# Shared small norm steps, outputs' norms on ACT, later bias additions, and K made beside P, in a macaron S4D block

## The chip, the cores and the metric

The kernel runs on one core of one Trainium2 chip. The metric is the device time of one execution in microseconds (us), taken as a median of several runs. A core has five engines that run side by side, each from its own queue in order: TensorE (PE, with its weight loads PEld), VectorE (DVE), ScalarE (ACT), GpSimd (POOL) and SyncE (SP, which here issues nearly all transfers). They meet through semaphores.

## The reference

The input x has 8 sequences of 2048 tokens with 256 features. Three sublayers follow one another, each added to its input:

```python
x = x + 0.5 * ffn(layernorm(x), w1, b1, w2, b2)
x = x + s4d(layernorm(x), log_A_real, A_imag, C_re, C_im, log_dt, D, ln_w, ln_b)
x = x + 0.5 * ffn(layernorm(x), w1, b1, w2, b2)
# ffn(x) = relu(x @ w1 + b1) @ w2 + b2, 256 -> 1024 -> 256
# s4d: K[h, l] = 2 Re sum_n Ct[h, n] exp(dt A[h, n] l);  y = causal convolution of x with K per feature
#      r = x + y + D x;  out = layernorm(r) * ln_w + ln_b
```

All of it is float32.

## The kernel before

**Stages.** There are 16384 tokens, cut into 64 groups of 256 (two tiles of 128 tokens on the partitions). The first feed-forward (tag "a") runs over the 64 groups, then comes the state-space stage, then the second feed-forward (tag "b"). The products are made to nearly float32 accuracy out of two parts of each operand (high and low, fp32r), three matmuls for one. The state-space stage works on 128-token chunks: its convolution needs the taps K of one chunk (kept in `kpad` in DRAM) and, for each batch of eight features, matrices P (kept turned in `pt_dram`) and O (`o_dram`) that take inputs into states and states into outputs.

**Steps.** `sublayer` (L821) writes out the work of a feed-forward in steps; a group has eight (`SLOTS`), one for each 128 columns of the hidden layer. In each step PE gets six matmuls of `up` (L802) and six of `down` (L812), which lags three steps (`LAG`). ACT makes the relu hx (L870) and DVE its low part (L117, hx). Around the matmuls run generators: `pre(g)` starts `lead` steps ahead (18 in "a") and makes a group's input, `post(g)` takes its output. Each `yield` in them passes one step, so the number of yields says how many steps ahead something is issued.

**An input** (`pre_a`, `ffn_in`): load x (256 KB on SP), statistics (two bn_stats, two bn_aggr on DVE), a root on ACT (`root`), two reciprocals and two small scalar_tensor_tensor q on DVE (`rstds`), nb on DVE and two normalisations into xn on ACT (`norm`, L701). POOL adds half of the output bias to x (L733). xn is then turned: for groups 14 to 18 and from 44 on by a DMA through DRAM (`turn_by_dma`, planes of 16 bits), for the others by four PE transposes (L740), after which ACT makes xh and DVE xl. Groups that PE turns load seven steps (`XL`) later than those that the DMA turns.

**An output** (`post_a`): DVE adds the down product to x (L917), SP stores it as x1, then the same chain of statistics, root, reciprocals and q, and the normalised rows go into columns of the big tile u: on ACT for groups below 12 (`ACT_NORM`), on DVE from 12 on (L705). `posted` counts the groups that are through.

**Background.** Beside the first feed-forward runs `matrices()`, a generator that yields paces in us of planned time. `fill` takes from it until its planned time has caught up with 1.32 a step (10.56 a group). It first makes the discrete parameters on DVE and powers of them on POOL (tables pa, pb), then the taps K (L499 to L556: 32 two-input steps on DVE over four rounds, 32 matmuls, and 16 small DMAs from POOL's queue), then P and O in 32 batches of eight features at a pace of 8.0 a batch: `make` on POOL (six products, L583 to L593), `spread` (two copies of 16-bit planes, one on DVE and one on ACT, L603, and stores of the planes and of O), `turn` (a transposing DMA read, pinned), `transpose` (two copies back, one on DVE and one on ACT, L629, pinned in program order, and a store). The parts of successive batches overlap, so the loop has 35 passes of six yields. Two marks have due groups: "half" (after pass 18) at group 32, since the later outputs need the room in u, and "tables" at group 48; a mark that isn't reached by then is forced, all that is left before it being issued at once. Last comes `early()`, the first part of the state-space stage.

**Order.** Within the dependencies the order on each engine is planned when the kernel is built, with program order as the priority; `keep_in_program_order` pins an instruction, and `issue_after` keeps one behind another. SP's and POOL's queues hold their DMA issues in that same order.

Of the kernel before, what the change touches and what calls it, by code (L numbers as in the profile page):

```python
# [10 lines left out]
F32 = mybir.dt.float32  # L11
# [8 lines left out]
P = 128  # L20
# [23 lines left out]
def macaron_s4d_kernel(  # L44
# [202 lines left out]
    def matrices():  # L247
# [248 lines left out]

        GP, GD = 32, 8  # L499
        vz = room[2][:, 0 : 2 * GP * 2 * NA].rearrange("p (r g c a) -> p r g c a", r=2, g=GP, c=2)  # L500
        for c in range(2):
            V.memset(vz[c * N : (c + 1) * N, :, :, 1 - c, :].rearrange("p r g a -> p (r g) a"), 0.0)
        za, zb = (
            room[2][:, i * P : (i + 2) * P].rearrange("p (g a) -> p g a", a=NA) for i in (8, 10)
        )
        mine = cells[14][:, 0:GD]
        V.tensor_reduce(
            mine, ident.rearrange("p (g x) -> p g x", g=GD), op=ALU.add, axis=mybir.AxisListType.X
        )
        prod = room[2][:, 16 * P : 20 * P].rearrange("p (q b g) -> p q b g", b=NB, g=GD)  # L510
        kev = room[2][:, 20 * P : 20 * P + (GP // GD) * NB].rearrange("p (q b) -> p q b", b=NB)
        yield S1
        for gi in range(NPAIR // GP):
            gs = slice(gi * GP, (gi + 1) * GP)
            br = pb[:, 0, gs, 0:1].to_broadcast([P, GP, NA])
            bi = pb[:, 1, gs, 0:1].to_broadcast([P, GP, NA])
            ar, ai = pa[:, 0, gs, :], pa[:, 1, gs, :]
            V.tensor_mul(za, ar, br)
            V.tensor_mul(zb, ai, bi)
            yield S2  # L520
            for c in range(2):
                cp = slice(c * N, (c + 1) * N)
                V.tensor_sub(vz[cp, 0, :, c, ::-1], za[cp], zb[cp])
            yield S2
            V.tensor_mul(za, ar, bi)
            stt(zb, ai, -1.0, br, ALU.mult, ALU.mult)
            yield S2
            for c in range(2):
                cp = slice(c * N, (c + 1) * N)
                V.tensor_sub(vz[cp, 1, :, c, ::-1], zb[cp], za[cp])  # L530
            yield S2
            pk = bank("b", f"pk{gi}")
            for q in range(GP // GD):
                for ri in range(2):
                    nc.tensor.matmul(
                        pk[:, q * P : (q + 1) * P],
                        vz[:, ri, q * GD : (q + 1) * GD].rearrange("p g c a -> p (g c a)"),
                        pb[:, ri, gi * GP + q * GD : gi * GP + (q + 1) * GD, :],
                        start=(ri == 0),
                        stop=(ri == 1),  # L540
                    )
                yield 1.3
            V.tensor_mul(
                prod,
                pk.rearrange("p (q g b) -> p q b g", g=GD, b=NB)[:, :, ::-1, :],
                mine.unsqueeze(1).unsqueeze(1).to_broadcast([P, GP // GD, NB, GD]),
            )
            yield 1.3
            V.tensor_reduce(kev, prod, op=ALU.add, axis=mybir.AxisListType.X)
            yield 1.3  # L550
            for q in range(GP // GD):
                h0 = 2 * (gi * GP + q * GD)
                nc.gpsimd.dma_start(
                    out=kpad[h0 : h0 + 2 * GD, 0:P].rearrange("h (a b) -> h a b", b=NB),
                    in_=kev[:, q, :],
                )  # L556


        first = NBT // 2
# [36 lines left out]
        def spread(bt):  # L596

            pl = planes[:, bt % 2]
            pu = p_of(bt).bitcast(U16).rearrange("p (m w) -> p w m", w=2)
            for _ in range(DI):  # L600
                yield
            for w in range(2):
                P_DEINT[w](pl[:, w], pu[:, w])  # L603
            yield
            via = pv_dram[bt % 2]
            nc.sync.dma_start(out=via, in_=pl.rearrange("p w m -> p (w m)"))
            yield
            nc.sync.dma_start(out=o_dram[bt], in_=p_of(bt))
            yield
# [24 lines left out]
            yield  # L634

        planes = wpool.tile([P, 2, 2, BCH * P], U16, name="planes", tag="wE")
        P_DEINT = (V.tensor_copy, A_.copy)
        P_REINT = (V.tensor_copy, A_.copy)
        PY = 0
        BACK = 3  # L640
        DI = 2
        PX = 2
        PA = 8.0
        PB_ = 8.0
        PPIN = 1

        for bt in range(NBT + BACK):
            parts = []
            if 0 <= bt - BACK < NBT:
                parts.append(transpose(bt - BACK))  # L650
            if 0 <= bt - 2 < NBT:
                parts.append(turn(bt - 2))
            if 0 <= bt - 1 < NBT:
                parts.append(spread(bt - 1))
            if bt < NBT:
                parts.append(make(bt))
            for n in range(6):
                for p in parts:
                    next(p, None)
                yield (PA if bt <= first else PB_) / 6  # L660
            if bt == first + BACK - 1:
                yield "half"
        yield "tables"
# [1 line left out]

    x1_dram = dram.tile([P, NJ * B, H], F32, name="x1_dram")

    def stats(srcs, name, pin=False):
        st = stat.tile([P, NTB, 6], F32, name=f"st_{name}", tag="st")
        mv = stat.tile([P, NTB, 2], F32, name=f"mv_{name}", tag="mv")  # L670
        for i, src in enumerate(srcs):
            ins = V.bn_stats(st[:, i, :], src)  # L672
            if pin:
                tc.keep_in_program_order(ins)
        for i in range(NTB):
            V.bn_aggr(mv[:, i, :], st[:, i, :])
        return mv

    def root(mv, name):

        s = stat.tile([P, NTB], F32, name=f"s_{name}", tag="s")
        A_.activation(s, mv[:, :, 1], AF.Sqrt, bias=eps4, scale=0.25)  # L682
        return s

    def rstds(mv, s, name):

        t = stat.tile([P, NTB], F32, name=f"t_{name}", tag="tt")
        q = stat.tile([P, NTB], F32, name=f"q_{name}", tag="q")
        V.reciprocal(t, s)
        stt(q, mv[:, :, 1], EPS, t, ALU.add, ALU.mult)  # L690
        stt(q, q, 0.25, s, ALU.mult, ALU.add)
        V.reciprocal(t, q)
        return t

    def norm(dsts, srcs, mv, rs, name, on_act=False):
        if on_act:
            nb = stat.tile([P, NTB], F32, name=f"nb_{name}", tag="nb")
            stt(nb, mv[:, :, 0], -1.0, rs, ALU.mult, ALU.mult)
        for i, (dst, src) in enumerate(zip(dsts, srcs)):
            if on_act:  # L700
                A_.activation(  # L701
# [16 lines left out]
    def halves(xt):  # L718
        return [xt[:, i, :] for i in range(NTB)]

    def ffn_in(xt, name, on_act=False, by_dma=False):

        mv = stats(halves(xt), f"f{name}", PINF)
        yield
        s = root(mv, f"f{name}")
        yield
        rs = rstds(mv, s, f"f{name}")
        yield
        norm(
            [xn[:, i, 0 : H - 1] for i in range(NTB)], [xt[:, i, 0 : H - 1] for i in range(NTB)],  # L730
            mv, rs, f"f{name}", on_act,
        )
        G_.tensor_add(xt, xt, hb2.unsqueeze(1).to_broadcast([P, NTB, H]))  # L733
        yield
        if by_dma:
            return (yield from turn_by_dma(xn, name))
        pt = bank("t", f"pt_{name}")
# [83 lines left out]
    def sublayer(w1t, w2t, pre, post, lead, tag, first=(), background=(), due=()):  # L821
# [9 lines left out]
        last = {}  # L831

        def step():
            for key in list(running):
                try:
                    next(running[key])
# [59 lines left out]

    LAG = 3
    pend = {}
    posted = [0]
    xts = {}  # L900


    ACT_NORM = 12

    def pre_a(g):
        by_dma = g >= DMA_A and not DMA_X <= g < DMA_Y
        for _ in range(0 if by_dma else XL):
            yield
        xt = xts[g] = slot("x", [P, NTB, H], f"xa_{g}")
        nc.sync.dma_start(out=xt, in_=hbm(x, g))  # L910
        for _ in range(XY):
            yield
        return (yield from ffn_in(xt, f"a{g}", True, by_dma))

    def post_a(g, po):
        xt = xts.pop(g)
        V.tensor_add(xt, po, xt)  # L917
        yield
        nc.sync.dma_start(out=x1_dram[:, g * NTB : (g + 1) * NTB, :], in_=xt)
        mv = stats(halves(xt), f"u{g}")  # L920
        yield
        s = root(mv, f"u{g}")
        yield
        rs = rstds(mv, s, f"u{g}")
        norm(ucols(g), halves(xt), mv, rs, f"u{g}", g < ACT_NORM)
        yield
        yield
        posted[0] = g + 1

# [155 lines left out]
    def early():  # L1085
# [41 lines left out]
    nc.gpsimd.dma_start(out=hb2, in_=b2.partition_broadcast(P))  # L1127
    G_.tensor_scalar_mul(hb2, hb2, 0.5)
    sublayer(
        w1t, w2t, pre_a, post_a, 11 + XL, "a", load_weights(), chain(matrices(), early()),  # L1130
        {"half": NG // 2, "tables": NG * 3 // 4},
    )

# [27 lines left out]

    def pre_b(g):
        by_dma = g >= DMA_B
        for _ in range(0 if by_dma else XL):
            yield
        xt = xts[g] = slot("x", [P, NTB, H], f"xb_{g}")
        i0 = g * NTB
# [21 lines left out]
    def post_b(g, po):  # L1189
# [7 lines left out]
        )  # L1197

    sublayer(
        [wb1[:, i] for i in range(2)], [wb2[:, i] for i in range(2)], pre_b, post_b, 12 + XL, "b"  # L1200
    )


# [30 lines left out]
```

## Time and profile before

| what | value |
|---|---|
| median of 3 runs | 1845.31 us (1841.72 to 1846.10) |
| the profiled execution's own time | 1843.95 us |
| its span, first to last instruction | 1842.2 us |
| mean granted TensorE clock | 0.98 |
| first feed-forward, relus of "a" | 20.9 to 854.5 us |
| second feed-forward, first to last `up` of "b" | 1094.3 to 1834.4 us |
| matmuls of each feed-forward | 6144 |

The page gives, for each engine, the time with an instruction in work, in all and in 40 equal slices of 46 us (each digit is a share in tenths). A row of a group reads: line, engine, operation, output <- inputs, shape, count, then busy us, mean ns of one, and the engine's idle time just before with what ended it. The idle time of an engine that isn't the bound costs nothing. A duration is that of an instruction in work, waits for a port included; instructions of one engine can overlap a little.

### The profile page before, as it was taken

What the parts mean: (1) busy time and instruction counts of PE and PEld (TensorE: products, weight loads), DVE (VectorE), ACT (ScalarE), POOL (GpSimd) and SP (SyncE); (2) the same over time, 40 slices, a digit from 0 to 9 for tenths busy, and PEclk for the clock granted to TensorE, in tenths of its full rate; (3) what the DMA queues carried; (4) which work ended last, traced back from release to release, by engine and by line L of the source; (5) the groups of instructions that cost most, each with busy time, mean ns of one, the idle gap of its engine ahead of it and who ended that gap; (6) DMA issues with size and microseconds to landing.
All of it is one profiled execution on the core that took longest, in us unless ns stands there. A gap on an engine that the chain in (4) does not pass through costs nothing. (4 is left out here: it accounts for less than half of the span.)

```text
span 1842.2 us, 41540 instructions
## 1 busy us (share of the span) xinstructions
PE 1747.9 (95%) x15147; PEld 1715.8 (93%) x15147; DVE 1492.6 (81%) x4919; ACT 925.2 (50%) x2139; POOL 713.7 (39%) x964
## 2 busy tenths in 40 slices
PE   6999799998998999999989879999999999999999
PEld 5999799988998999998888879999999999999998
DVE  5999897888899867765999947888888888888875
ACT  4455334554655655553545425555555555555553
POOL 1116851888587414111778612222222222222220
PEclk9999899998999999999999979999999999999999
DMA  5112132787888933334878833333332333333332
GB/s 203 47 47 56 52 111 77 241 237 227 247 250 246 247 110 90 101 105 137 253 232 235 256 115 87 93 89 92 88 100 85 91 98 87 98 89 90 94 95 55
DMA packets 299696, 246.39 MB, mean 134 GB/s; under 512 B 169954, under 2 KB 242402, under 8 KB 298978
## 3 DMA queue, kind: packets, MB, share of 16 engines
q1 hardware_dynamic: 297456, 241.75, 45.2%
q8 instruction: 119, 1.95, 0.4%
q10 hardware_dynamic: 1266, 1.31, 0.2%
q0 software_dynamic: 768, 0.66, 0.2%
q14 instruction: 87, 0.71, 0.1%
HBM read 92.93 MB, written 111.15 MB: 111 GB/s over the span
## 5 line engine op out<-in xcount | busy, mean ns | idle before, releaser
L812 PE MATMUL po_a<-wa,hx_a 128*128 128x256 f32 x3072 | 457.1, 287 | 17.4 <-DVE hx_a L117 17.1
L802 PE MATMUL ph_a<-xh_a,wa 128*128 128x256 f32 x2048 | 460.2, 289 | 5.2 <-ACT xh_a L749 3.5
L802 PE MATMUL ph_b<-xh_b,wb 128*128 128x256 f32 x2048 | 443.2, 284 | 2.5 <-ACT xh_b L749 2.4
L812 PE MATMUL po_b<-wb,hx_b 128*128 128x256 f32 x3072 | 441.2, 283 | 0.3 <-DVE hx_b L117 0.3
L812 PEld LDWEIGHTS po_a<-wa,hx_a 128*128 128x128 f32 x3072 | 407.7, 194 | 23.4 <-DVE hx_a L117 22.4
L812 PEld LDWEIGHTS po_b<-wb,hx_b 128*128 128x128 f32 x3072 | 400.5, 192 | 0.5 <-DVE hx_b L117 0.5
L802 PEld LDWEIGHTS ph_a<-xh_a,wa 128*128 128x128 f32 x2048 | 361.3, 196 | 6.8 <-ACT xh_a L749 3.9
L802 PEld LDWEIGHTS ph_b<-xh_b,wb 128*128 128x128 f32 x2048 | 352.8, 193 | 3.6 <-ACT xh_b L749 3.0
L802 PE MATMUL ph_a<-xl_a,wa 128*128 128x256 f32 x1024 | 294.1, 290 | 23.4 <-DVE xl_a L751 20.6
L870 ACT ACTIVATE hx_b<-ph_b 128x256 fp32r<-128x256 f32 x512 | 191.6, 381 | 244.3 <-PE ph_b L802 226.6
L117 DVE SCALAR_TENSOR_TENSOR hx_a<-ph_a,hx_a 128x256 fp32r<-128x256 f32 x512 | 207.9, 412 | 127.7 <-ACT hx_a L870 126.6
L870 ACT ACTIVATE hx_a<-ph_a 128x256 fp32r<-128x256 f32 x512 | 189.0, 381 | 228.8 <-PE ph_a L802 213.6
L1169 POOL TENSOR_TENSOR xb<-xb,lnb_sb 128x512 f32<-128x512 f32 x64 | 84.0, 1315 | 523.3 <-DMA xb<-x_dram 384.4
L802 PE MATMUL ph_b<-xl_b,wb 128*128 128x256 f32 x1024 | 285.2, 284 | 0.0
L117 DVE SCALAR_TENSOR_TENSOR hx_b<-ph_b,hx_b 128x256 fp32r<-128x256 f32 x512 | 210.1, 414 | 57.3 <-ACT hx_b L870 51.7
L802 PEld LDWEIGHTS ph_a<-xl_a,wa 128*128 128x128 f32 x1024 | 201.2, 196 | 27.0 <-DVE xl_a L751 23.5
L733 POOL TENSOR_TENSOR xa<-xa,hb 128x512 f32<-128x512 f32 x64 | 85.5, 1336 | 362.4 <-ACT xn L701 328.0
L802 PEld LDWEIGHTS ph_b<-xl_b,wb 128*128 128x128 f32 x1024 | 197.4, 193 | 0.2 <-DVE xl_b L751 0.2
L701 ACT ACTIVATE xn<-xa,nb_fa,t_fa 128x255 f32<-128x255 f32 x128 | 69.7, 591 | 104.2 <-DVE nb_fa L117 82.2
L733 POOL TENSOR_TENSOR xb<-xb,hb 128x512 f32<-128x512 f32 x64 | 93.9, 1467 | 50.0 <-ACT xn L701 34.5
L701 ACT ACTIVATE xn<-xb,nb_fb,t_fb 128x255 f32<-128x255 f32 x128 | 69.9, 594 | 75.7 <-DVE nb_fb L117 72.0
L761 DVE COPY pl_b<-xn 128x512 uint16<-128x512 uint16 x62 | 42.7, 688 | 74.3 <-ACT xn L701 74.3
(264 smaller groups left out, 2773.2 us busy)
## 6 DMA issues: line engine op xcount, KB each, us to landing
xa<-in_L_attn_x_dram SPq DMA_DIRECT2D x64, 256.0 KB, 2.9
x_dram<-xa SPq DMA_DIRECT2D x64, 256.0 KB, 2.3
o<-u SPq DMA_DIRECT2D x32, 512.0 KB, 4.2
pv<-planes SPq DMA_DIRECT2D x32, 512.0 KB, 3.6
pt<-u SPq DMA_DIRECT2D x32, 512.0 KB, 3.3
tz<-kpad SPq DMA_DIRECT2D x64, 256.0 KB, 4.2
xb<-x_dram SPq DMA_DIRECT2D x64, 256.0 KB, 2.7
out_dram<-xb SPq DMA_DIRECT2D x64, 256.0 KB, 2.9
```

The costliest lines, as they stand in the source:

```text
L117: return V.scalar_tensor_tensor(out=o, in0=a, scalar=s, in1=b, op0=op0, op1=op1)
L701: A_.activation(dst, src, AF.Identity, bias=nb[:, i : i + 1], scale=rs[:, i : i + 1])
L733: G_.tensor_add(xt, xt, hb2.unsqueeze(1).to_broadcast([P, NTB, H]))
L761: copy(pl[:, w], xu[:, :, :, :, w])
L802: nc.tensor.matmul(ph, wt[wp][:, dc, fs], xp[:, dc, :], start=(n == 0), stop=(n == 3 * NDC - 1))
L812: nc.tensor.matmul(po[:, i, :], hp[:, tsl], wt[wp][:, fc, :], start=(fc == 0 and i == 0 and n == 0), stop=(fc == NFC - 1 and n == 2), skip ...
L870: last[A_] = A_.activation(hh, ph, AF.Relu)
L1169: G_.tensor_add(xt, xt, lnb_sb.unsqueeze(1).to_broadcast([P, NTB, H]))
```

## The change

Only the first feed-forward and what runs beside it are edited.

1. K's code becomes a generator `lags()`. It is no longer run ahead of P: one yield of it is taken with each of the six yields of a pass of P's loop, and its own paces aren't counted.
2. Both copies of P's deinterleave (`spread`) are on ACT, one a yield. P's paces go from 8.0 to 9.1 for the first 19 passes and to 10.3 after that.
3. From group 3 on, the statistics of an input g and those of the output g-3 lie in one tile (class `Joint`). `post_a(g-3)` makes one root, one set of reciprocals and q, and one nb for both; `ffn_in(g)` waits three yields and uses them. `post_a` has no yield any more between the addition and the store, and one between nb and the norms.
4. `ACT_NORM` goes from 12 to 52, so ACT normalises the outputs of groups 12 to 51 too.
5. With a joint, the bias addition is put into a generator of its own that waits five more steps, and is pinned in program order on POOL.
6. Inputs from group 3 on are all loaded at the same distance ahead; groups that PE turns wait two more steps after the norm instead.

The lead stays at 18 and 19, and the second feed-forward keeps its numbers.

```diff
-        GP, GD = 32, 8
...
-                nc.gpsimd.dma_start(
-                    out=kpad[h0 : h0 + 2 * GD, 0:P].rearrange("h (a b) -> h a b", b=NB),
+        def lags():
+            GP, GD = 32, 8
...
             for w in range(2):
-                P_DEINT[w](pl[:, w], pu[:, w])
-            yield
+                A_.copy(pl[:, w], pu[:, w])
+                yield
...
-        PA = 8.0
-        PB_ = 8.0
+        PA = 9.1
+        PB_ = 10.3
...
+        beside = lags()
...
                 for p in parts:
                     next(p, None)
-                yield (PA if bt <= first else PB_) / 6
+                next(beside, None)
+                yield (PA if bt < first + BACK else PB_) / 6
...
+    def shifts(mv, rs, name):
+        nb = stat.tile([P, mv.shape[1]], F32, name=f"nb_{name}", tag=f"nb{mv.shape[1]}")
+        stt(nb, mv[:, :, 0], -1.0, rs, ALU.mult, ALU.mult)
+        return nb
...
+    def ffn_in(xt, name, on_act=False, by_dma=False, joint=None):
+
+        if joint:
+            stats(halves(xt), f"f{name}", mv=joint.mv[:, 0:NTB])
+
+            for _ in range(3):
+                yield
+            mv, rs, nb = joint.mv[:, 0:NTB], joint.rs[:, 0:NTB], joint.nb[:, 0:NTB]
...
-        G_.tensor_add(xt, xt, hb2.unsqueeze(1).to_broadcast([P, NTB, H]))
-        yield
+        def add_bias():
+            return G_.tensor_add(xt, xt, hb2.unsqueeze(1).to_broadcast([P, NTB, H]))
+
+        def later():
+            for _ in range(5):
+                yield
+            tc.keep_in_program_order(add_bias())
+
+        if joint:
+            spawned.append((name, later()))
+        else:
+            add_bias()
+        yield
+        if joint and not by_dma:
+            yield
+            yield
...
-    ACT_NORM = 12
+    ACT_NORM = 52
...
+    class Joint:
+        def __init__(self, g):
+            self.mv = moments(2 * NTB, f"j{g}")
+
+    joints = {}
+    JG = 3
...
-        for _ in range(0 if by_dma else XL):
+        for _ in range(XL if g < JG else 0):
             yield
...
+        if g >= JG:
+            joints[g - JG] = Joint(g - JG)
+        return (yield from ffn_in(xt, f"a{g}", True, by_dma, joints.get(g - JG)))
...
         V.tensor_add(xt, po, xt)
-        yield
         nc.sync.dma_start(out=x1_dram[:, g * NTB : (g + 1) * NTB, :], in_=xt)
-        mv = stats(halves(xt), f"u{g}")
-        yield
-        s = root(mv, f"u{g}")
-        yield
-        rs = rstds(mv, s, f"u{g}")
-        norm(ucols(g), halves(xt), mv, rs, f"u{g}", g < ACT_NORM)
-        yield
+        joint = joints.pop(g, None)
+        mv = stats(halves(xt), f"u{g}", mv=joint.mv[:, NTB:] if joint else None)
+        whole = joint.mv if joint else mv
+        yield
+        s = root(whole, f"u{g}")
+        yield
+        rs = rstds(whole, s, f"u{g}")
+        nb = shifts(whole, rs, f"u{g}")
+        if joint:
+            joint.rs, joint.nb = rs, nb
+            rs, nb = rs[:, NTB:], nb[:, NTB:]
+        yield
+        norm(ucols(g), halves(xt), mv, rs, f"u{g}", g < ACT_NORM, nb)
         yield
         posted[0] = g + 1
```

## The prediction

> **What bounds the kernel now.** I read the page first: busy times, and the 40 slices of 46 us.
>
> ```profile
> PE 1747.9 (95%) x15147; PEld 1715.8 (93%) x15147; DVE 1492.6 (81%) x4919; ACT 925.2 (50%) x2139; POOL 713.7 (39%) x964
> ...
> PE   6999799998998999999989879999999999999999
> PEld 5999799988998999998888879999999999999998
> DVE  5999897888899867765999947888888888888875
> ACT  4455334554655655553545425555555555555553
> POOL 1116851888587414111778612222222222222220
> ```
>
> PE is the bound, but not evenly. The second feed-forward (slices 24 on) is full; the first (14 to 855 us) has holes, just where POOL's row is high. Only the first is edited, so I look at its groups. The time line has eight hx_a activations on ACT for each group of 256 tokens; the first of groups 1, 11, 15, 21, 23, 43, 44 and 48 start at 36.5, 155.3, 219.1, 300.5, 324.4, 597.1, 617.0 and 663.2 us. I asked for the busy time in these stretches:
>
> ```profile
> 36.50:155.30 118.80, 118.80 (x995) 118.44 (x995) 107.28 (x435) 59.84 (x149) 20.36 (x22) 1.00 0.15 45
> 155.30:219.10 63.80, 55.98 (x428) 54.93 (x426) 55.87 (x151) 28.18 (x70) 52.72 (x47) 0.92 0.21 63
> 219.10:300.50 81.40, 76.59 (x626) 74.86 (x627) 73.92 (x213) 31.64 (x82) 39.57 (x42) 1.00 0.24 79
> 324.40:597.10 272.70, 250.46 (x1992) 244.47 (x1991) 243.57 (x633) 148.76 (x316) 210.99 (x172) 0.97 0.80 240
> 597.10:617.00 19.90, 16.89 (x120) 16.18 (x121) 17.67 (x44) 8.90 (x19) 14.91 (x12) 0.92 0.82 235
> ```
>
> Columns: length, then busy PE, PEld, DVE, ACT, POOL, clock, DMA share, GB/s. Groups 1 to 10 take 11.88 us each with PE full, although DVE is 90% busy. The **floor** of a group is 11.52 us (the chain of waits repeats at that step in the second feed-forward), plus 0.45 for four transposes where the input isn't turned by DMA: 11.97. Groups 23 to 42, with the tables P made beside them, take 13.63 us. There I asked for the waits between 330 and 610 us (total, times, longest):
>
> ```profile
> ACT xn L701 <- DVE nb_fa L117: 61.7, 19, 5.4
> POOL xa L733 <- ACT xn L701: 33.6, 14, 10.9
> ...
> PE ph_a L802 <- DVE xl_a L751: 16.7, 12, 3.0
> ```
>
> So PE waits for DVE, ACT stands at its queue's head for nb_fa with the relus behind it, and POOL stands behind ACT. Why DVE is late shows in the groups by form, first in that window, then in 760 to 800 us, where POOL is nearly idle:
>
> ```profile
> L705 DVE TENSOR_SCALAR u<-xa,mv_u,t_u 128x256 f32<-128x256 f32 x40 | 33.3, 928 | 0.1
> L603 DVE COPY planes<-u 128x1024 uint16<-128x1024 uint16 x27 | 27.3, 1012 | 0.0
> L117 DVE SCALAR_TENSOR_TENSOR q_u<-mv_u,t_u 128x2 f32<-128x2 f32 x20 | 12.2, 612 | 0.3
> L117 DVE SCALAR_TENSOR_TENSOR q_u<-q_u,s_u 128x2 f32<-128x2 f32 x20 | 11.4, 570 | 0.2
> ```
>
> ```profile
> L705 DVE TENSOR_SCALAR u<-xa,mv_u,t_u 128x256 f32<-128x256 f32 x6 | 2.7, 550 | 0.0
> L117 DVE SCALAR_TENSOR_TENSOR q_u<-mv_u,t_u 128x2 f32<-128x2 f32 x3 | 0.5, 161 | 0.1
> ```
>
> The same step on two numbers takes 161 ns alone and 612 beside POOL. The time line shows how; nb_fa ends as POOL's operation does, and ACT, which starts 0.1 us after it, has stood 8.75 us (put down to "issue"):
>
> ```profile
> 215.04 2.97 DVE L117 SCALAR_TENSOR_TENSOR nb_fa<-mv_fa,t_fa 128x2 f32<-128x2 f32 x1
> ...
> 216.93 1.06 POOL L583 TENSOR_TENSOR u<-u 128x512 f32<-128x512 f32 x1
> ...
> 218.09 1.09 ACT L701 ACTIVATE xn<-xa,nb_fa,t_fa 128x255 f32<-128x255 f32 x2 [8.75 <-issue]
> ```
>
> **The change, part by part** (durations from 330 to 610 us, 20 groups).
>
> Shared small steps. For groups 3 on, one root, two reciprocals, two q and one nb serve an input (g) and an output (g-3) together. On DVE that takes away one q pair, 0.61 + 0.57 us, and one reciprocal pair, 0.16 + 0.14: 1.48 us a group; on ACT one root of 0.29. The steps left work on four numbers instead of two; I take the same duration. New is a wait: an input's norm now needs the outputs of group g-3. By the step counts these are added at step 8g-14, the norms run at 8g-11, and the input is used at 8g. A late nb holds ACT's head and the relus behind it; PE has three steps, 4.3 us, before it misses hx.
>
> Outputs' norms on ACT to group 51. DVE loses 2 x 0.93 = 1.86 us a group, ACT gains 2 x 0.84 = 1.68 (row of u<-xa,nb_u, 18 before 150 us). The Trainium skill, "ScalarE: Activation LUTs", Rules for kernel authors, would keep plain arithmetic off ACT; by DVE's 550 ns alone it would be right here, by the 928 beside POOL it is not, and the difference decides only the ACT rival below.
>
> Both copies of P's deinterleave on ACT: DVE loses 1.01 us, ACT gains 1.05, per batch. P's paces go from 8.0 to 9.1 and 10.3 units; a group is 8 x 1.32 = 10.56, so batches a group fall from 1.32 to 1.16, then 1.03. Groups 23 to 42 then hold 21 batches instead of 26.
>
> The bias addition waits five more steps and leaves POOL's head: the 33.6 us of POOL waits vanish. Behind it on POOL stand P's products. It comes at 8g-5 and is needed at 8g+10, 21 us on; free. If POOL were stuck behind a kpad DMA or a pt store (11.3 us of such waits in all), those 21 us still cover it.
>
> Loads of groups 3 to 13 and 19 to 43 are issued seven steps earlier, and the store of x1 one step earlier, right behind the addition. On SP the store can hold what follows (pv, planes, pt) until DVE has added; now SP waits 12.8 us in all for that addition in the 280 us. Hidden by the batch period of 10.4 us against landings of 3 to 5; uncovered it would come back as ACT's pinned waits for planes, 8.0 us now. The earlier loads cost five x buffers nothing: 31 steps of life against 40.
>
> The uniform timing also removes two bursts. Today groups 14 and 44 normalise 11 steps ahead but 13 and 43 four ahead, so two groups' inputs fall into one group's time: groups 13, 14 and 43 last 15.8, 20.9 and 19.9 us. And xl, ready one step ahead now, is ready six ahead, so the 16.7 us wait goes.
>
> K beside P. K's own pauses, 0.9 + 4 x 13.2 = 53.7 units, go, so P begins that much earlier; K's DVE work (its rows sum to 30 us), its 64 matmul records (14 take 1.73 us, so 7.9) and its 16 POOL DMAs stand among the first seven batches, six groups instead of five. These DMAs now stand in POOL's queue between products (6.7 us of waits for DVE now). No row shows K beside P: from nothing lost to each of 32 two-input steps waiting 0.45 (0.61 less 0.16), 14 us. The Trainium skill, "GPSIMD Engine Reference", Key points, says that POOL and DVE share SBUF interfaces and that DVE instructions with two SBUF inputs contend; the 161 and 612 ns agree, and by it the upper end is the one to expect.
>
> Does DVE still bind in groups 23 to 42? Rows left: hx 64.7, add 13.6, xl 13.5, statistics 31.7, aggregates 11.2, q 23.6, nb 6.1, reciprocals 6.3, reinterleave 21 x 1.18 = 24.8: 196 us; today's rows sum to 291. Rows overlap (291 against 251 merged, 0.86), so 168 of about 244: 69%, below the 90% at which groups 1 to 10 held the floor. ACT: hx 57.5, xn 22.9, xh 11.6, roots 6, u 33.6, deinterleave 44, reinterleave 29: 205, merged by 0.89 to 182, 75%, plus waits. So PE, with some friction:
>
> - groups 11 to 14: floor 47.4, now 63.8; I take 52 (the rows save 4 x 3.3, and the burst): 11.8 gained
> - groups 15 to 20: floor 77.9 with K, now 81.4; I take 83.4: 2.0 lost (nearer to no loss, since DVE sheds 3.3 a group here too)
> - groups 21 and 22: now without P at 23.9, then with: 0.6 lost
> - groups 23 to 42: floor 239.4, now 272.7; at 12.2 each 244: 28.7 gained
> - group 43: 19.9 to 12.2: 7.7 gained
> - the rest, the state-space stage and the second feed-forward: nothing, their instructions stay.
>
> Sum 45.6 us. The profiled execution took 1843.95 us (span 1842.2), 1.4 below the median: 1798, told against the median **1799**. With every group at its floor 61 us go: 1783.
>
> **Rivals.**
> 1. DVE still binds through K and the contended steps: all 14 us of K are paid, and groups 23 to 42 recover half, at 12.8: 1844 - 11.8 + 14 + 0.6 - 16.7 - 7.7 = 1822. For it: q and nb stay contended, POOL is fuller under K. Against: 69%.
> 2. Groups 23 to 42 are set by the transfers (DMA 0.80) and SP's waits, and stay at 13.63; the bursts alone go: 1844 - 11.8 + 2.6 - 7.7 = 1827. Against: PE's waits there name DVE, none a DMA.
> 3. **Slower**: ACT becomes the bound, in order. It would work 182 / 20 = 9.1 us a group; its waits for nb, s and planes are now (61.7 + 23.7 + 4.9 + 8.0) / 20 = 4.9. With both norms behind one later nb, waits over 5.3 make groups 23 to 43 cost more than the other parts gain (21 x 14.4 = 302 against 293 + 9). If every nb wait were the longest seen, 5.4, it is 7.2; halfway, 6.2, gives 21 x 15.3 = 321, or 1844 + 28 - 9 = 1863. Against: nb loses four of the contended steps ahead of it.
> 4. The emitted order undoes it (P forced at the mark "half", due at 259 steps x 1.32 = 342 units. Now P is there at 217 + 19 x 8 = 369 and is forced; after, at 163 + 19 x 9.1 = 336): nothing, 1844.
>
> **How the numbers follow.** Forecast 0.65, rival 1 0.13, rival 2 0.08, rival 3 0.10, rival 4 0.04. Less than 0.3%, 5.5 us, can't be told from no change here. So faster 0.86, same 0.04, slower 0.10. The range runs from 1780 (the floor of 1783, less 3 us by which runs differ) to 1830, past rivals 1 and 2, and leaves out rivals 3 and 4 and the tails.
>
> **What would show it.** Right: groups 23 to 42 near 12.2 us, PE's waits for xl gone, ACT's busy share there near 75%, DVE's near 69%, no long group 14 or 43, P's last store some 60 us before 644. Wrong: ACT waiting for nb over 5 us a group and PE for hx (rival 3); groups 15 to 20 over 15 us (rival 1); planes waits grown (rival 2); changes after 855 us.

## The result and the profile after

The changed kernel takes 1836.69 us in the median (19 runs, 1830.44 to 1842.89), the kernel before beside it 1844.28 (19 runs). The ratio is 0.9958, with a 95% interval of 0.9948 to 0.9968: some 8 us faster, where 45 were forecast. The profiled execution took 1839.24 us, its span is 1837.5; every profile below is of one execution, and the 19 of this kernel lie up to 12 us apart.

The page of the changed kernel, busy times and slices:

```profile
PE 1745.1 (95%) x15147; PEld 1713.1 (93%) x15147; DVE 1401.9 (76%) x4554; ACT 994.9 (54%) x2190; POOL 705.1 (38%) x964
...
PE   5999999989989899999999879999999999999999
...
DVE  5898887766765656665999947888888788888884
ACT  3454466767766666553545425555555555555553
```

DVE's row has fallen from between 7 and 9 to between 5 and 7 in slices 7 to 14, and ACT's has risen there to 6 and 7: the work moved as the prediction's rows said. PE's row hardly changed. So the question is not whether DVE was relieved, but what took its place. The busy time in the same groups as before (11 to 14, 15 to 20, 23 to 42, 43):

```profile
157.70:216.20 58.50, 52.97 (x413) 52.29 (x412) 47.03 (x116) 29.22 (x65) 46.24 (x43) 0.94 0.20 55
216.20:308.30 92.10, 83.38 (x653) 80.95 (x652) 73.02 (x189) 53.00 (x105) 63.47 (x59) 0.96 0.56 167
...
335.10:595.00 259.90, 243.52 (x1992) 238.80 (x1992) 175.00 (x483) 180.05 (x346) 172.93 (x146) 1.00 0.74 220
595.00:613.00 18.00, 13.70 (x93) 12.70 (x92) 10.82 (x34) 10.55 (x21) 6.94 (x6) 0.83 0.77 218
```

In groups 23 to 42 no engine behind PE is busy for more than 69% of the time (DVE 67, ACT 69, POOL 67), and still a group takes 13.0 us. The stretch got 12.8 us shorter. Only 5.9 us of this are idle time of PE's (22.2 us before, 16.4 now). The other 6.9 are PE's busy time, and they go with the granted clock, 0.97 in the row before and 1.00 here (an estimate: 0.03 of 272.7 us is some 8). Groups 15 to 20 got 10.7 us longer. PE's wait for hx before, between 330 and 610 us, and the waits after, between 310 and 595 us:

```profile
PE po_a L812 <- DVE hx_a L117: 6.2, 10, 1.9
```

```profile
DVE hx_a L117 <- ACT hx_a L907: 66.9, 41, 3.6
POOL xa L754 <- ACT xn L712: 37.1, 13, 12.7
ACT hx_a L907 <- PE ph_a L836: 36.9, 47, 1.4
ACT xn L712 <- DVE nb_u L117: 24.2, 17, 4.7
...
PE po_a L846 <- DVE hx_a L117: 13.8, 19, 1.3
```

ACT's waits for nb fell (61.7 to 24.2 us), and PE no longer waits for xl. In their place DVE now waits 67 us for ACT's relu (24 before), and PE stands behind both, 13.8 us for hx. The time line shows the relu's place in ACT's queue, in a typical group:

```profile
535.33 0.38 ACT L907 ACTIVATE hx_a<-ph_a 128x256 fp32r<-128x256 f32 x1 [0.99 <-PE ph_a L836]
537.92 1.09 ACT L712 ACTIVATE xn<-xa,nb_u,t_u 128x255 f32<-128x255 f32 x2 [2.20 <-DVE nb_u L117]
538.92 1.44 ACT L712 ACTIVATE u<-xa,nb_u,t_u 128x256 f32<-128x256 f32 x2
540.15 1.38 ACT L630 COPY u<-planes 128x1024 uint16<-128x1024 uint16 x1
541.40 0.37 ACT L907 ACTIVATE hx_a<-ph_a 128x256 fp32r<-128x256 f32 x1
541.67 1.03 ACT L604 COPY planes<-u 128x1024 uint16<-128x1024 uint16 x1
542.60 0.38 ACT L907 ACTIVATE hx_a<-ph_a 128x256 fp32r<-128x256 f32 x1
```

```profile
542.28 0.98 PE L846 MATMUL po_a<-wa,hx_a 128*128 128x256 f32 x6 [0.66 <-DVE hx_a L117]
```

Between two relus ACT waits 2.2 us for nb, then runs the inputs' norms, the outputs' norms that the change gave it, and the pinned copy of P's reinterleave: 5.7 us from 535.7 to 541.4. PE bears about 4.3 us, an estimate from the three steps of 1.44 us (an eighth of 11.52) by which `down` lags. It stalls, although ACT is idle elsewhere in the group.

In group 43 the pinned copy itself waits at the queue's head, for the transposed planes:

```profile
600.89 0.39 ACT L907 ACTIVATE hx_a<-ph_a 128x256 fp32r<-128x256 f32 x1 [0.93 <-PE ph_a L836]
603.82 1.34 ACT L630 COPY u<-planes 128x1024 uint16<-128x1024 uint16 x1 [2.55 <-DMA planes<-pv]
605.03 1.08 ACT L712 ACTIVATE xn<-xa,nb_u,t_u 128x255 f32<-128x255 f32 x2
606.02 1.39 ACT L712 ACTIVATE u<-xa,nb_u,t_u 128x256 f32<-128x256 f32 x2
607.22 0.40 ACT L907 ACTIVATE hx_a<-ph_a 128x256 fp32r<-128x256 f32 x1
```

```profile
608.13 1.65 PE L846 MATMUL po_a<-wa,hx_a 128*128 128x256 f32 x6 [3.74 <-DVE hx_a L117]
```

All that has been ready since 602 us stands behind a transfer, and the next relu comes six us after the last. PE's longest wait, 3.74 us, ends there. The six matmuls right after it take 1.65 us, where six took 0.88 at 600.63; the granted clock of the group is 0.83. So this stall cost more than its own length.

### The profile page after: what moved, and what is told of

It reads as the page before. It is cut to its first block, busy times and chain, and to the rows that moved or that the text cites. A ratio compares the mean times of both kernels' runs of the same rounds, so it can differ in the third digit from the quotient of the medians.

```text
span 1837.5 us, 41268 instructions
## 1 busy us (share of the span) xinstructions
PE 1745.1 (95%) x15147; PEld 1713.1 (93%) x15147; DVE 1401.9 (76%) x4554; ACT 994.9 (54%) x2190; POOL 705.1 (38%) x964
## 5 line engine op out<-in xcount | busy, mean ns | idle before, releaser
L846 PE MATMUL po_a<-wa,hx_a 128*128 128x256 f32 x3072 | 463.3, 288 | 30.3 <-DVE hx_a L117 29.3
L795 DVE COPY pl_b<-xn 128x512 uint16<-128x512 uint16 x62 | 47.2, 761 | 74.3 <-ACT xn L712 74.3
L712 ACT ACTIVATE xn<-xa,nb_u,t_u 128x255 f32<-128x255 f32 x122 | 66.6, 593 | 37.9 <-DVE nb_u L117 33.8
```

The costliest lines, as they stand in the source:

```text
L712: A_.activation(dst, src, AF.Identity, bias=nb[:, i : i + 1], scale=rs[:, i : i + 1])
L795: copy(pl[:, w], xu[:, :, :, :, w])
L846: nc.tensor.matmul(po[:, i, :], hp[:, tsl], wt[wp][:, fc, :], start=(fc == 0 and i == 0 and n == 0), stop=(fc == NFC - 1 and n == 2), skip ...
```

## The experiments

Ratios are to the kernel before, measured on the same chip. "Groups" below are read from each profiled time line by its relus (eight a group), as before, one execution each.

**Undoing one move at a time.** First the outputs' norms:

```diff
-    ACT_NORM = 52
+    ACT_NORM = 12
```

> The changed kernel with ACT_NORM back at 12, so DVE makes the outputs' norms of groups 12 to 51 again. Theory A (ACT's queue: relus stand behind one unbroken run of nb wait, xn, u and the pinned reinterleave): taking the 1.44 us of u out of that run shortens it from about 5 us to 3.6, under the 4.3 us that PE bears, so groups 23 to 42 fall from 13.0 to about 12.5 and the time by some 10 us to 1827. Theory B (DVE's relief is what the change lives on): DVE gets 1.86 us a group back beside POOL, groups 23 to 42 rise to 13.4 or more, the time goes back to 1845.

Ratio 0.9886 (0.9870 to 0.9901), 1821.4 us: 13 us faster than the changed kernel by the ratios, so with the other edits in place the move to ACT costs. Groups 23 to 42 took 12.70 us. DVE is busier than in the changed kernel, and PE faster:

```profile
330.20:584.20 254.00, 244.32 (x2005) 241.60 (x2005) 212.03 (x527) 158.45 (x308) 172.47 (x146) 0.99 0.76 226
```

DVE stands at 83% and ACT at 62%. Theory B falls for this kernel.

One deinterleave copy back on DVE:

```diff
-                A_.copy(pl[:, w], pu[:, w])
+                P_DEINT[w](pl[:, w], pu[:, w])
...
+        P_DEINT = (V.tensor_copy, A_.copy)
```

> The changed kernel with one of the two deinterleave copies of each batch back on DVE. Theory A (ACT's queue): ACT loses 1.04 us a batch out of the same run, groups 23 to 42 fall from 13.0 to about 12.6, the time by 8 us to 1829. Theory B (DVE's relief): DVE gets about 1.0 us a batch back, groups 23 to 42 at 13.2, the time 1841.

Ratio 0.9930 (0.9916 to 0.9944), 1830.1 us. The direction is theory A's, about 5 us, but groups 23 to 42 only fell to 12.91 and their relus were as late as before; this run alone proves little.

K ahead of P again, at the old paces:

```diff
-        PA = 9.1
-        PB_ = 10.3
+        PA = 8.0
+        PB_ = 8.0
...
-        beside = lags()
+        yield from lags()
+        beside = iter(())
```

> The changed kernel with K run ahead of P again at its own paces, and P's paces at 8.0 as before. Theory C (K beside P costs what the rest gains): groups 15 to 22, 118.9 us now and 105.3 before, fall by some 10 us, and the time to 1827; the stretch from 23 on stays near 13.0. Theory A: that stretch holds more batches a group and gets slower (13.4), about what K gives back, and the time stays within 4 us of 1837.

Ratio 0.9949 (0.9926 to 0.9973), 1832.6 us, not told apart from the changed kernel's 0.9958. Groups 11 to 22 took 171.8 instead of 177.3 us, groups 23 to 42 266.8 instead of 260.0. K beside P costs early and gives back later, through its slower paces; here it is a wash.

The same work in another order:

```diff
         yield
+        if joint:
+            yield
+            yield
         norm(ucols(g), halves(xt), mv, rs, f"u{g}", g < ACT_NORM, nb)
```

> The changed kernel with the outputs' norms issued two steps after the inputs' norms instead of right behind them; the work on each engine is the same, only the order on ACT differs. Theory A (the unbroken run on ACT): the run loses 1.44 us, relus pass between, groups 23 to 42 fall to about 12.5, time 1827. Theory D (ACT's total work sets it): no change, 13.0 and 1837 within 3 us.

Ratio 0.9943 (0.9929 to 0.9957), 1832.1 us; groups 23 to 42 at 12.62. The stretch did what theory A said, but an edit that changes next to no work, further down, brought it to 12.60 too. The total fell by only 3 us.

**Each part by itself.** What is left with both moves undone and K ahead at the old paces (the shared steps, the uniform distance, the later bias):

> The changed kernel with the outputs' norms (groups 12 to 51) and one deinterleave copy back on DVE, and K ahead of P at the old paces: what is left is the shared small steps, the uniform load distance and the later bias addition. Theory A (shared steps gain, work moved to ACT gives it back): about 1822, near all that DVE's norms brought in the last runs. Theory B (shared steps alone bring little, DVE stays the bound at about 290 less 30 us of rows in 20 groups): about 1835. K unimportant: within 4 us of the run that keeps K beside P.

Ratio 0.9987 (0.9976 to 0.9997), 1842.3 us: next to nothing. Theory B is nearer, and even it expected more.

Both moves undone, K beside P:

> The changed kernel with the outputs' norms and one deinterleave copy back on DVE, K still beside P. If ACT's queue is all there is: 1815 or less, groups 23 to 42 at 12.4, since both moves to ACT are undone (they brought 15 and 7 us alone). If DVE becomes the bound again: its rows rise by 1.86 and about 1.1 us a group, groups 23 to 42 at 13.0 and the time near 1828, above the 1821 with only the norms on DVE.

Ratio 0.9936 (0.9921 to 0.9952), 1833.2 us; groups 23 to 42 at 12.64. Slower by 9 us than with the norms alone on DVE, which speaks for the first move off DVE: ACT's queue isn't all. The next two runs show that from the other side. On the kernel before, only ACT_NORM at 52:

> The kernel before with ACT_NORM at 52 alone, so ACT makes the outputs' norms of groups 12 to 51. Theory A: relus stand behind longer runs, slower by 5 to 15 us, 1850 to 1860. Theory B (DVE is the bound there, 90% busy and late with nb): 1.86 us a group less on DVE, faster by 10 to 25 us, 1820 to 1835.

Ratio 0.9921 (0.9905 to 0.9937), 1829.9 us, 14.5 us faster. Theory B holds here. And only the deinterleave, both copies on ACT:

> The kernel before with both deinterleave copies on ACT alone. Theory A: slower or the same, 1843 to 1850. Theory B: DVE loses 1.0 us a batch, 1.3 a group over 22 groups, faster by 10 to 20 us, 1825 to 1835.

Ratio 0.9967 (0.9955 to 0.9980), 1838.1 us, 6 us faster, less than B's 10. So each move helps a kernel whose DVE is full, and in the changed kernel the two together do not add up. By the ratios, the deinterleave on ACT gains 9 us with the outputs' norms on DVE (0.9936 to 0.9886) and loses 5 with them on ACT (0.9930 to 0.9958). Each of these two differences is no larger than what edits further down moved without a known cause (4 and 9 us).

**What joins them.** The run in the time line ends in the pinned copy, so that one copy was unpinned, on ACT alone:

```diff
-                if PPIN:
+                if PPIN and w == 0:
                     tc.keep_in_program_order(ins)
```

> The changed kernel with ACT's copy of the reinterleave no longer pinned in program order. Theory A (both moves together fill ACT's run between relus): the planner can put it among the relus, faster than 1837 by 4 to 10 us. Theory D (ACT's order is set by nb and the planner's view of time, not by the pin): same order, within 3 us of 1837.

Ratio 0.9863 (0.9843 to 0.9882), 1817.1 us: 17.5 us faster than the changed kernel by the ratios, with no work added or taken away. The groups that correspond:

```profile
328.40:571.90 243.50, 241.88 (x2014) 240.54 (x2014) 168.74 (x483) 180.34 (x348) 169.75 (x146) 1.00 0.78 233
```

```profile
PE po_a L846 <- DVE hx_a L117: 0.8, 2, 0.6
```

20 groups in 243.5 us, 12.17 each, with ACT's 180 us of work as in the changed kernel (and a larger share, 74%, of a shorter time). PE's wait for hx (second fence, from 335 to 570 us) is all but gone, and PE is idle for 1.6 us instead of 16.4, at the same clock of 1.00. The planner now puts the copy between relus:

```profile
493.26 0.38 ACT L907 ACTIVATE hx_a<-ph_a 128x256 fp32r<-128x256 f32 x1 [1.06 <-PE ph_a L836]
493.54 1.37 ACT L630 COPY u<-planes 128x1024 uint16<-128x1024 uint16 x1
494.76 0.29 ACT L688 ACTIVATE s_u<-mv_j,eps 128x4 f32<-128x4 f32 x1
494.96 0.37 ACT L907 ACTIVATE hx_a<-ph_a 128x256 fp32r<-128x256 f32 x1
496.20 0.38 ACT L907 ACTIVATE hx_a<-ph_a 128x256 fp32r<-128x256 f32 x1 [0.87 <-PE ph_a L836]
498.05 1.09 ACT L712 ACTIVATE xn<-xa,nb_u,t_u 128x255 f32<-128x255 f32 x2 [1.47 <-DVE nb_u L117]
499.05 1.44 ACT L712 ACTIVATE u<-xa,nb_u,t_u 128x256 f32<-128x256 f32 x2
500.28 0.42 ACT L907 ACTIVATE hx_a<-ph_a 128x256 fp32r<-128x256 f32 x1
```

The norms' run is 3.7 us with its wait, under 4.3. Counted over groups 23 to 42, from one relu's start to the next:

| kernel | group, us | steps over 4.3 us | their excess, us | PE's wait for hx, us | ratio |
|---|---|---|---|---|---|
| before | 13.63 | 14 | 18.8 | 5.3 | 1 |
| changed | 13.00 | 15 | 19.9 | 13.5 | 0.9958 |
| outputs' norms two steps later | 12.62 | 10 | 11.3 | 6.4 | 0.9943 |
| paces 9.2 and 10.4 (below) | 12.60 | 16 | 16.1 | 7.2 | 0.9938 |
| outputs' norms on DVE | 12.70 | 3 | 3.4 | 6.6 | 0.9886 |
| ACT's reinterleave unpinned | 12.17 | 4 | 3.8 | 0.8 | 0.9863 |

Of the changed kernel's 15 long steps 13 hold the outputs' norms, 11 the pinned copy, nine both. But the count of long steps doesn't set the time: the kernel before has 14 (there PE waits another 16.7 us for xl), the new paces 16. In the five changed versions the group's time follows PE's own wait much more closely. New paces alone lead to 12.60; of the other edits, only the unpinning goes below that.

Is it the pin as such, or only the pin together with the moved work? The same edit on the kernel before, and on the changed kernel with its outputs' norms on DVE:

> The kernel before with ACT's reinterleave copy unpinned. Theory A (the pin costs because the change puts the outputs' norms and a second deinterleave ahead of the pinned copy): here, without them, it brings little, 1838 to 1845. Theory E (the pin costs in any case, the change has nothing to do with it): faster by the same 20 us, about 1823.

> The changed kernel with ACT's reinterleave unpinned and the outputs' norms on DVE. Theory A (norms and pinned copy form one run on ACT; either edit breaks it): no more than the unpinned one alone, 1817 to 1822. Theory E: the two gains add, 20 + 15 us, about 1803.

Ratios 1.0011 (0.9999 to 1.0022) and 0.9887 (0.9867 to 0.9908). Against 1 and 0.9886 the unpinning brings nothing in either. Theory E falls: the pin's 17.5 us are not there without the outputs' norms on ACT. Whether they are there whenever these norms are is another matter: with K ahead of P, the last run below, the same unpinning brings 3.5 us by the ratios, with overlapping intervals (0.9949 and 0.9930).

**Smaller questions.** ACT makes the norms of even groups only (`g < 12 or (g < ACT_NORM and g % 2 == 0)`):

> The changed kernel with ACT making the outputs' norms of even groups alone from 12 on, DVE those of odd ones. Theory A (a run of about 5 us on ACT, over the 4.3 that PE bears): half of the groups lose the long run, so the time lies between 1821 (all on DVE) and 1837 (all on ACT), about 1829. If instead the balance of total work sets it: DVE and ACT then stand at about 74 and 66% and the time falls below both, 1818.

Ratio 0.9911 (0.9894 to 0.9927), 1826.8 us: in between, as theory A had it, though by differences of 6 to 9 us.

The outputs' norms on DVE and the bias addition nine steps later instead of five:

> The changed kernel with the outputs' norms back on DVE and the bias addition four steps later still (nine instead of five). POOL stands behind ACT's xn for 37 us between 310 and 595 us although the addition was put later. If that wait matters to PE: 4 to 8 us faster than the 1821 of the same kernel with five steps. If POOL isn't on the path: within 3 us of 1821, with the waits of the addition on xn gone.

Ratio 0.9935 (0.9918 to 0.9953), 1831.9 us, 9 us slower than with five steps. Neither reading foresaw that. POOL's waits for xn are smaller (11.7 us between 335 and 590, against 15.8) but not gone, PE's for hx larger (24.0 against 17.5 between 155 and 663). Why is open; it may be the plan alone.

The kernel before with the outputs' norms on ACT and K beside P (K's code and paces as in the changed kernel):

> The kernel before with the outputs' norms on ACT to group 51 and K beside P at the new paces, without shared steps and without the other edits. The same with shared steps and the rest, one deinterleave copy on DVE, took 1830. If the shared steps and the uniform distance bring what the rows said, 1.5 us a group and the bursts: 1845 or more. If they bring nothing beside a relieved DVE: 1825 to 1832.

Ratio 0.9941 (0.9928 to 0.9954), 1831.2 us. The shared steps and all that goes with them, with one deinterleave copy on each engine, give 0.9930: no more than 2 us between them.

What a new plan does by itself:

```diff
-        PA = 9.1
-        PB_ = 10.3
+        PA = 9.2
+        PB_ = 10.4
```

> The changed kernel with P's paces at 9.2 and 10.4, an edit that changes next to no work and only makes the plan anew. It measures what a new plan alone does to the time. If the plan is steady: within 3 us of 1837. If not: up to 10 us off, and differences of that size between two kernels here are no proof of a cause.

Ratio 0.9938 (0.9922 to 0.9954), 4 us from the changed kernel, for a hundredth more pace. In its profile, the fastest of its six executions, groups 23 to 42 take 12.60 us each instead of 13.00, 8 us less in the stretch. With the 9 us of the bias run, this says what may be read here: the 13 and 17.5 us above are beyond it, the 13 not by much; differences of 2 to 9 are not proof by themselves, and neither is a stretch at 12.6.

K ahead of P, with ACT's copy unpinned:

> The changed kernel with ACT's reinterleave unpinned and K ahead of P at P's old paces. Theory C (K beside P costs 5 to 13 us in groups 11 to 22, the slower paces give 7 to 15 back after): those groups near 169 us instead of 175, groups 23 to 42 near 12.7 instead of 12.2, time 1817 to 1824. If the paces were not needed once ACT's run is broken: 1810.

Ratio 0.9930 (0.9912 to 0.9948), 1830.2 us: 12 us slower than with K beside P. Groups 11 to 22 gained 0.9 us (173.7 against 174.6), groups 23 to 42 took 12.88 each instead of 12.17. With this copy unpinned K beside P pays, which is more than theory C allowed; that it pays through the slower paces that it makes possible is the likely reading, no run changes the paces alone by as much.

The fastest version tried is the changed kernel with that one copy unpinned, 1817.1 us, and it beats both kernels.

## Why the prediction was wrong

The direction was right; 45 us were forecast and 8 came. In the profiles, of the 45.6 forecast, groups 11 to 22 miss 17.4 us (a gain of 9.2 forecast, a loss of 8.2 measured), groups 23 to 42 miss 15.9 (28.7 and 12.8), group 43 misses 5.8 (7.7 and 1.9) and groups 44 to 47, where nothing was counted, lose 2.6. So that the sum still came out as a gain owes something to luck. Its steps, one by one:

**The bound before** was read rightly: with DVE full, one move off it gave 14.5 us, another 6, each alone on the kernel before.

**The shares** came out as summed: DVE 69% forecast, 67 measured; ACT 75% forecast, 69 measured, and 74 once the stretch ran at the forecast's 12.17.

**The step that failed** in groups 23 to 42 is the sentence that DVE at 69% was "below the 90% at which groups 1 to 10 held the floor", with ACT's 75% "plus waits", and so 12.2 us a group. Groups 1 to 10 had PE full with an ACT whose relus were never more than 3.1 us apart. An in-order queue isn't read by its share: on ACT a wait for nb, four norms and one pinned copy follow one another, and the relu that PE needs every 1.44 us stands behind all of them. PE waited 13.5 us for hx, where the forecast had some friction, and groups 23 to 42 took 260 us instead of 244. With the copy unpinned the wait was 0.8 us and they took 243.5, so the forecast of the stretch held for a kernel that differs by one pin. Rival 3 had the place (both norms behind one nb, in ACT's order) and the wrong price: it counted waits per group against total work, and asked for over 5 us of them for nb. ACT waited 1.1 us a group for nb, and still PE waited for hx, the other half of that rival's sign.

**Group 43** was to lose its burst, 7.7 us. It lost 1.9: the two inputs no longer fall together, but the pinned copy waits there for its transfer. Unpinned it takes 14.5 us (with the copy pinned and the outputs' norms on DVE, 13.6).

**K beside P** and the groups around it: 159.9 us were forecast for groups 11 to 22, before 169.1, measured 177.3. This is the second step that failed, a term too small, and the largest part of the miss. In four pairs of runs K beside P, with the paces that go with it, lengthens these groups by 5.5, 10.0, 13.1 and 0.9 us, so the 2.6 us that I took were too small in three of them. Rival 1's sign, groups 15 to 20 over 15 us, appeared: they took 15.4 each. But its mechanism didn't. The 32 two-input steps of K sum to 21.4 us beside P and to 23.8 in the kernel before; none of the 14 us that they were to wait shows there. PE's idle time in these groups rose by only 1.9 us (12.6 to 14.5), and a lower granted clock in groups 15 to 20 (1.00 before, 0.96 after) accounts for some 3 us of their 10.7. What makes up the rest stays open. The 11.8 us gained in groups 11 to 14 became 5.3. With K ahead, groups 11 to 22 took 168 to 174 us in every variant, about what they take in the kernel before: it may be that what is done sooner there only lets the next background work begin sooner. That the background refills a gap is argued from these sums, no run isolates it.

**Shared small steps**: 1.48 us a group less on DVE were counted, at the old durations. The rows after, from 330 to 610 us:

```profile
L117 DVE SCALAR_TENSOR_TENSOR q_u<-q_u,s_u 128x4 f32<-128x4 f32 x22 | 15.0, 682 | 0.3
L117 DVE SCALAR_TENSOR_TENSOR q_u<-mv_j,t_u 128x4 f32<-128x4 f32 x22 | 12.5, 567 | 0.5
L117 DVE SCALAR_TENSOR_TENSOR nb_u<-mv_j,t_u 128x4 f32<-128x4 f32 x22 | 12.3, 561 | 0.7
```

The steps that are left still wait for POOL, nb more than before (561 ns against 306). These rows and the reciprocals sum to 2.15 us a group, before to 2.97: 0.8 us were saved. With the uniform distance and the later bias, but without the moves, they changed the time by 0.13%.

**The bias addition** didn't leave POOL's head: POOL waits 37.1 us for xn (310 to 595 us), before 33.6 (330 to 610). The pin puts it five steps on in the plan, but ACT's norm is late by more. The one run on it went the other way. But in the fastest version POOL waits 44.1 us for xn between 335 and 570 us while PE waits 0.8 us for hx, so this wait of POOL's need not hold PE.

**xl** came as forecast: PE's waits for the PE-turned xl fell from 20.6 us to 4.6 in all. P's last store was forecast some 60 us before 644; the first came 60 us earlier (263 instead of 323) but the last at 641.8, since the slower paces take back the earlier start, which I had counted as fewer batches a group and not as a later end. The second feed-forward changed by about 1 us (740.1 to 738.9, first to last `up`), as good as nothing, as forecast.

## What to carry to other kernels

When work moves to an engine that another engine waits for every step, don't ask for its share of busy time; write down what will stand in its queue between two of those steps, waits included, and compare the longest run with the slack (here 5.7 us against 4.3). Take the price from what the bound engine itself waits for, not from the number of such runs. A pinned instruction that was harmless can become the last link of such a run when other work is put before it, so moves and pins are tested together: the pin was worth 0 us before, 0 with one move, 17.5 with both, and 3.5 with both and K ahead. And where a planner orders the queues, measure what an empty edit does (here 4 us in all, 8 in one stretch) before reading a small difference as a cause.

## What the runs showed of the hardware that I had not expected

A DVE step on [128 x 4] beside POOL's products takes as long as one on [128 x 2], 561 to 682 ns against 570 to 612 for the outputs' q before; 0.15 to 0.16 us for the same steps when POOL isn't in the way (nb_u at 601.79 us in the changed kernel took 0.15). So halving the number of such steps could have halved the loss, but nb, which had been cheap at 306 ns, now takes 561 in the mean, as the steps beside POOL do.
